# Loading x alone first, ten sigmoid tiles, weight means moved into the layer norm, one set of banks, and VectorE in the first two Sobel pairs

## The chip, the core and the metric

The kernel runs on one core of one Trainium2 chip. A core has a matrix engine (TensorE, called PE in the profile), a vector engine (VectorE, DVE), a scalar engine (ScalarE, ACT) and a general engine (GpSimd, POOL). SyncE (SP) only issues DMA transfers here. Every engine works off its own queue of instructions in order, and waits on semaphores for the others. TensorE writes its products to PSUM, which holds eight banks of 128 partitions by 512 float32. The metric is the device time of one execution in microseconds (us). All data is float32.

## The reference

Four layers on one image x of 256 x 256 pixels with 32 channels, each with its residual:

```python
x = x + attention(_gn(x))   # layer 0
x = x + sobel(_gn(x))       # layer 1
x = x + sobel(_gn(x))       # layer 2
x = x + recurrent(_gn(x))   # layer 3
```

`_gn` normalizes 16 groups of two channels over the whole image. `attention` normalizes each pixel over its 32 channels (mean, variance, `ln_gamma`, `ln_beta`), and then makes `q`, `k`, `v` and `g = sigmoid(mn @ Wg)` with 256 columns each. The softmax runs over an axis of length 1, so its weights are 1, and what is left is

```python
o = g * (mn @ Wv)
return o @ Wo + bo
```

`sobel` takes a 3 x 3 average (edges divided by the number of pixels that count), the two 3 x 3 Sobel gradients per channel, and `sqrt(gx*gx + gy*gy + 1e-6)`. `recurrent` takes the rows of the image as 256 sequences of 256 steps with 32 features, and runs two LSTM-like cells of 128 units with a group norm (four groups, `gn_gamma`, `gn_beta`) on the 512 gate inputs of each cell. For inputs whose `gn_gamma` is all ones and `gn_beta` all zeros the kernel takes a branch without these factors; a test of the two arrays sets `flag`, by which the branch is chosen.

## The kernel before

The image lies in SBUF as `xa`: 128 partitions are four neighbouring columns of the image (J = 4) times 32 channels, and the free side is 64 blocks (NB) of 256 rows. Work goes by *pairs* of blocks (128 x 512 elements), 32 of them (NST). From the load to the end of the Sobel layers the order of the instructions on each engine is the order in which the program writes them (`manual_schedule`); no scheduler moves them.

*Load.* SP loads x in natural layout into tiles `nat` and `half` (WIDTHS: two of 16 columns, then seven of 32; two DMAs each). TensorE transposes 128 x 128 pieces into PSUM (`pt`), ScalarE copies each pair into `xa` (L254), VectorE takes its statistics (`bn_stats`, L255). ScalarE's queue loads `kg` (two 128 x 128 matrices: group averaging and channel centring) and `mean_of`; GpSimd's queue loads the weights, `ln_gamma` and `ln_beta`, four times over. In the last third of the load `weights()` puts four narrow products and two of 128 x 256 on TensorE: the bias that `ln_beta` gives, and the centred weights `wv4` and `wg4`.

*Group norm and layer norm.* `bn_aggr`, two products with `kg` that average over a group (`pm`, `pv`), and from them `less` (minus the mean) and `scale`. `shifted(k)` subtracts the mean from a pair (mostly VectorE, L284). Eight groups of four pairs follow: TensorE centres each over channels (`pc`, L346), ScalarE squares (L369), TensorE sums the squares into `pvar` (L327). ScalarE's square root and VectorE's reciprocal (L360 for the first group of pairs, L376 for the others) make `rstd`. `rows_of(k)` has SP spread row `k` of `rstd` over 128 partitions, in four DMAs of 64 KB into one of three `rows` buffers (L305); `scaled(k)` multiplies a pair by it (pair 0 on VectorE, others on GpSimd, L315). `norm_test` (L744 to L747) compares `gn_gamma` and `gn_beta`, laid out on one partition, and writes `flag`. PSUM is split into a pool of seven banks for `pc` and one for `pvar`.

*Attention.* A list `plan` gives each step of a pair a planned time, with 5.9 between pairs; all pairs' entries, sorted by planned time, are the program. Per pair: eight products with `wv` (v) and eight with `wg` (g) on TensorE in 32-row slices (L441), eight sigmoids on ScalarE (`sg`, L450), eight times `o = (v + bias) * sg` on VectorE (L454), two groups of four products with `wo` (`pr`, `pb`, L467) into one bank, ScalarE's copy `r` with the bias `bo` (L482), GpSimd's addition into `xa` (L483), and `bn_stats` (L486). Banks are taken first in, first out from a list of eight; `sg` tiles from a list of eight and `o` tiles from a list of eleven. `spread_out` (the rows' DMAs) of pair k is planned five pairs ahead, `scaled` two pairs ahead.

`RecurrentWeights` is created where the attention starts: SP loads `wc` (2 x 512 KB, L758), GpSimd clears `bc` (L762), SP loads a row of it (L763). Its `centring()` gives a list of small instructions, one of which is put into each pair of the attention: reduces on VectorE (L809, L813: means of `bc` and `wc` by gate group) and subtractions on GpSimd (L816).

*Sobel layers.* A list `parts` with planned times 3.6 apart, sorted in the same way. Per pair: `convert` (ScalarE, into PSUM), `twos` and `threes` (VectorE, L586, L601), `ends` (ScalarE), then on GpSimd `fours` (L606), `difference` (L614) and `smooth` (L610), then two groups of products on TensorE (`mixed`, L648), squares, sum, root, residual and statistics. At the head of a layer `shift()` makes the group mean and then has TensorE multiply 16 idle products (L561); `deviation()` makes the scale.

*Recurrence.* 256 steps over two cells, with the weights that `rw.finish` makes ready. The change leaves it as it is.

Of the kernel before, what the change touches and what calls it, by code (L numbers as in the profile page):

```python
# [18 lines left out]
S = 256  # L19
T = 256  # L20
C = 32
# [40 lines left out]
def net_kernel(  # L62
# [35 lines left out]
    nc.scalar.dma_start(out=kg, in_=consts[:, 0:2, :])  # L98
# [18 lines left out]
    gamma4 = cp.tile([P, 1], F32, name="gamma4")  # L117
    beta4 = cp.tile([P, 1], F32, name="beta4")
    wv4 = big2.tile([P, D], F32, name="wv4")
    wg4 = big2.tile([P, D], F32, name="wg4")  # L120
    for t, v in (
        (wv4, w_v),
        (wg4, w_g),
        (gamma4, ln_gamma.rearrange("(c o) -> c o", o=1)),
        (beta4, ln_beta.rearrange("(c o) -> c o", o=1)),
    ):
        for j in range(J):
            nc.gpsimd.dma_start(out=t[j * C : (j + 1) * C, :], in_=v)
# [8 lines left out]
    one = eps_tile(1.0, "one")  # L137
# [52 lines left out]
    mean_of = mp.tile([P, P], F32, name="mean_of")  # L190
    nc.scalar.dma_start(out=mean_of, in_=consts[:, K_AVG, :])
    flag = cp.tile([1, 1], mybir.dt.int32, name="flag")
    stats = new_stats()
    def pair(t, k):
        return t[:, 2 * k : 2 * k + 2, :].rearrange("p b s -> p (b s)")
# [3 lines left out]
    WIDTHS = [16, 16] + 7 * [32]  # L199
    w0 = 0  # L200
    with tc.tile_pool(name="nat", bufs=7, side="right") as natp, tc.tile_pool(
        name="ps_in", bufs=5, space=PSUM
    ) as ps_in:
        nats = []
        for i, wl in enumerate(WIDTHS):
            name, bufs = ("nat", 7) if wl == 32 else ("half", 2)
            nat = natp.tile([P, 2, wl, C], F32, name=name, bufs=bufs)
            nats.append((nat, w0, wl))
            for h in range(2):
                nc.sync.dma_start(out=nat[:, h], in_=x_nat[:, h, w0 : w0 + wl, :])  # L210
            w0 += wl
        nc.sync.dma_start(out=kt, in_=consts[:, 3:NK, :])
        gb = norm_weights(tc, mp, gn_gamma, gn_beta)
        nc.gpsimd.memset(avg, 0.0)
        for g in range(GROUPS):
            nc.gpsimd.tensor_copy(avg[:, g, g, :], mean_of[:, 0:P:C])
        scaled_w = []
        for w in (wv4, wg4):
            scaled_w.append(mp.tile([P, D], F32, name="wgam", bufs=2))
            nc.gpsimd.tensor_scalar(scaled_w[-1], w, gamma4, None, ALU.mult)  # L220

        def weights():

            pbias = ps_in.tile([P, 2, 2, P], F32, name="pt")
            for i, w in enumerate((wv4, wg4)):
                for half in range(2):
                    nc.tensor.matmul(
                        pbias[:, i, half, 0:1],
                        lhsT=w[0:C, half * P : (half + 1) * P],
                        rhs=beta4[0:C, :],  # L230
                        start=True,
                        stop=True,
                    )
            nc.scalar.copy(wbias, pbias[:, :, :, 0:1].rearrange("p i h o -> p i (h o)"))
            for w, wg in zip((wv4, wg4), scaled_w):
                pw = ps_in.tile([P, 2, 2, P], F32, name="pt")
                pw = pw[:, 0].rearrange("p h s -> p (h s)")
                nc.tensor.matmul(pw, lhsT=kg[:, K_CEN, :], rhs=wg, start=True, stop=True)
                nc.scalar.copy(w, pw)

        for i, (nat, w0, wl) in enumerate(nats):
# [14 lines left out]
            if i == len(nats) - 3:  # L256
                weights()
# [6 lines left out]
    with tc.tile_pool(name="ps_gn", bufs=1, space=PSUM) as ps_gn:  # L264
        mv = small.tile([P, nc.vector.BN_AGGR_DIM], F32, name="mv")
        nc.vector.bn_aggr(mv, stats)
        busy(ps_gn, 5)
        pm = ps_gn.tile([P, 1], F32, name="pm")
        nc.tensor.matmul(pm, lhsT=kg[:, K_GN, :], rhs=mv[:, 0:1], start=True, stop=True)
        less = small.tile([P, 1], F32, name="less")  # L270
        nc.vector.tensor_scalar_mul(less, pm, -1.0)
        d = small.tile([P, 1], F32, name="d")
        nc.vector.tensor_add(d, mv[:, 0:1], less)
        q = small.tile([P, 1], F32, name="q")
        nc.vector.scalar_tensor_tensor(q, d, d, mv[:, 1:2], ALU.mult, ALU.add)
        pv = ps_gn.tile([P, 1], F32, name="pv")
        nc.tensor.matmul(pv, lhsT=kg[:, K_GN, :], rhs=q, start=True, stop=True)
        busy(ps_gn, 3)
        nc.scalar.activation(pair(xb, 2), pair(xa, 2), AF.Identity, bias=less)
        gstd = small.tile([P, 1], F32, name="gstd")  # L280
        nc.scalar.activation(gstd, pv, AF.Sqrt, bias=gn_eps)

        def shifted(k):
            nc.vector.tensor_scalar(pair(xb, k), pair(xa, k), one, less, ALU.mult, ALU.add)  # L284

        shifted(0)
        shifted(1)
        scale = small.tile([P, 1], F32, name="scale")
        nc.vector.reciprocal(scale, gstd)
        nc.vector.tensor_scalar(cen, kg[:, K_CEN, :], scale, None, ALU.mult)  # L290
        shifted(3)
        for w in (wv4, wg4):
            nc.scalar.activation(w, w, AF.Copy, scale=scale)

    def pair(t, k):
        return t[:, 2 * k : 2 * k + 2, :].rearrange("p b s -> p (b s)")
# [20 lines left out]
    with tc.tile_pool(name="lnq", bufs=9) as lnq:  # L317
        with tc.tile_pool(name="ps_ln", bufs=7, space=PSUM) as ps_ln, tc.tile_pool(
            name="ps_var", bufs=1, space=PSUM
        ) as ps_var:  # L320
            pvars = []

            def variance(g, sqs):
                if g in (0, EARLY):
                    pvars.append(ps_var.tile([P, 2 * S], F32, name="pvar"))
                for j in range(J):
                    nc.tensor.matmul(  # L327
                        pvars[-1][j * C : (j + 1) * C, :],
                        lhsT=avg[:, g].rearrange("p k j -> p (k j)"),
                        rhs=sqs[j],  # L330
                        start=g in (0, EARLY),
                        stop=g in (EARLY - 1, GROUPS - 1),
                    )

            def deviations():
                std = lnq.tile([P, 2 * S], F32, name="std", bufs=1)
                nc.scalar.activation(std, pvars[-1], AF.Sqrt, bias=ln_eps)
                return std

            last = std = None  # L340
            for g in range(GROUPS):
                pcs = [ps_ln.tile([P, 2 * S], F32, name="pc") for _ in range(J)]
                for j in range(J):
                    rows = slice(j * C, (j + 1) * C)
                    for r in range(J):
                        nc.tensor.matmul(  # L346
                            pcs[j][r * C : (r + 1) * C, :],
                            lhsT=cen[rows, rows],
                            rhs=pair(xb, J * g + r)[rows],
                            start=True,  # L350
                            stop=True,
                        )
                if g == 0:
                    for k in range(J, 5 * J):
                        shifted(k)
                sqs = []
                for j, pc in enumerate(pcs):
                    if g == EARLY + 1 and j == 1:
                        std = deviations()
                        nc.vector.reciprocal(rstds[0], std)  # L360
                        for k in range(3):
                            rowsets[k] = rows_of(k)
                        for k in range(5 * J, NST):
                            shifted(k)
                        norm_test(tc, mp, flag, gb)
                        for k in range(3):
                            scaled(k)
                    sqs.append(lnq.tile([P, 2 * S], F32, name="sq"))
                    nc.scalar.activation(sqs[-1], pc, AF.Square)  # L369
                if g:  # L370
                    variance(g - 1, last)
                last = sqs
            variance(GROUPS - 1, last)
            std = deviations()
            table(AF.Sigmoid, std[:, 0:1])
            nc.vector.reciprocal(rstds[1], std)  # L376

    means.close()
    rw = RecurrentWeights(tc, cells, one, w_cell, b_cell)
# [38 lines left out]
        (22.5883, "bn", 0, 0),  # L418
    ]
    with tc.tile_pool(name="at", bufs=3) as atp, tc.tile_pool(  # L420
        name="ps_at", bufs=1, space=PSUM
    ) as ps_at:
        free = list(range(8))
        held, sbuf = {}, {}
# [85 lines left out]
        for _, f, args in todo:  # L510
            f(*args)
# [756 lines left out]
```

## Time and profile before

| | us |
|---|---|
| median of 3 runs | 2520.72 (2519.58 to 2522.09) |
| the profiled execution's own time | 2522.59 |
| its span in the profile | 2520.8 |
| PE busy in the span | 2476.7 (98%) |
| DVE busy | 2273.3 (90%) |
| ACT busy | 2256.1 (89%) |
| POOL busy | 1332.8 (53%) |

By stages, in us from the start of the span (busy time of each engine in the stage; the clock is the mean TensorE clock that was granted, 1 being full speed):

| stage | from, to | PE | DVE | ACT | POOL | clock |
|---|---|---|---|---|---|---|
| load | 0, 33 | 23.75 | 20.40 | 20.68 | 16.78 | 1.00 |
| group and layer norm | 33, 59 | 23.04 | 23.71 | 19.97 | 0.00 | 1.00 |
| attention | 59, 303 | 237.03 | 200.69 | 188.21 | 89.60 | 0.96 |
| Sobel, first | 303, 425 | 121.84 | 106.97 | 87.72 | 97.27 | 1.00 |
| Sobel, second | 425, 549 | 123.94 | 107.91 | 87.38 | 97.92 | 1.00 |
| group norm, weights | 549, 560 | 9.43 | 7.35 | 3.80 | 0.36 | 1.00 |
| recurrence | 560, 2520.8 | 1937.66 | 1806.30 | 1848.30 | 1030.88 | 0.99 |

In the lines of a timeline, the first number is the start of a run of like instructions on one engine, the second their busy time, then come the engine, the line of the program, the operation, output and inputs with their shapes, and how many there are. In square brackets stands how long the engine was idle before, and what ended the idle time: the engine, the tile and the line that it waited for. "SPq" is SP's queue, where DMAs are issued. A busy PE need not be PE at its peak: a matmul is shown from its start to its modelled end.

### The profile page before, as it was taken

Reading aid. Unit: us, or ns where it says so; the run is one execution under the profiler, and the core shown is the slowest. Engines: PE = TensorE matmul, PEld = TensorE weight load, DVE = VectorE, ACT = ScalarE, POOL = GpSimd, SP = SyncE. Lnnn points to the kernel's source line nnn. Section 1 sums busy time; section 2 is a strip of 40 time slices with the busy share of each in tenths; the row PEclk is TensorE's granted clock in tenths of the full one; section 3 lists DMA queues with packets and bytes.
Section 4 is the critical chain, followed back from the end, with each engine's and each line's share of the span. In section 5 each row is a group of like instructions: output and inputs, shape, how many; then the busy total and the mean of one; then the engine's idle time right before and its main releaser. Section 6 shows DMA issues by size and latency. Waiting matters only on the chain.

```text
span 2520.8 us, 41461 instructions
## 1 busy us (share of the span) xinstructions
PE 2476.7 (98%) x11593; PEld 1062.3 (42%) x11593; DVE 2273.3 (90%) x6635; ACT 2256.1 (89%) x6878; POOL 1332.8 (53%) x1368
## 2 busy tenths in 40 slices
PE   7999999999999999999999999999999999999997
PEld 4444445563444444444444444444444444444442
DVE  7688897977999999999999999999999999999996
ACT  6788676758999999999999999999999999999996
POOL 2334487854555555555555555555555555555553
PEclk9899999998999999999999999999999999999998
DMA  6777100010010101010100101010101010100000
GB/s 163 60 38 39 8 1 1 1 39 13 5 22 5 22 5 22 5 24 8 21 15 12 22 5 22 5 22 5 22 5 22 5 22 5 22 5 5 5 7 9
DMA packets 117449, 46.98 MB, mean 19 GB/s; under 512 B 76964, under 2 KB 110021, under 8 KB 117208
## 3 DMA queue, kind: packets, MB, share of 16 engines
q1 hardware_dynamic: 115032, 43.60, 13.0%
q8 instruction: 95, 1.56, 0.3%
q14 instruction: 146, 1.20, 0.2%
q10 hardware_dynamic: 1376, 0.33, 0.1%
q0 software_dynamic: 800, 0.30, 0.1%
HBM read 10.63 MB, written 8.39 MB: 8 GB/s over the span
## 4 chain that ended last, share of the span: by engine, by line
PE 76%; DVE 0%; ACT 0%; issue 0%; POOL 0%; POOLq 0%; ACTq 0%; DVEq 0%
PE zz L1086 37%; PE zz L1081 17%; PE zz L1054 9%; PE pt L1138 5%; PE zz L1051 3%; PE pt L1134 2%; PE px L1183 1%; PE px L1173 1%; POOL rs L1102 0%; DVE ve L1099 0%; ACT ga L1075 0%; ACT sq L1094 0%; PE px L1166 0%; DVE c L1122 0%; ACT go L1075 0%
## 5 line engine op out<-in xcount | busy, mean ns | idle before, releaser
L1102 POOL TENSOR_TENSOR rs<-ve,mhalf 128x4 f32<-128x4 f32 x1024 | 1030.9, 1007 | 924.7 <-DVE ve L1099 924.7
L1086 PE MATMUL zz<-wc,hT 128*128 128x512 f32 x2040 | 1060.4, 607 | 0.7 <-DVE hT L1144 0.7
L1075 ACT ACTIVATE ga<-zz,rs 128x128 f32<-128x128 f32 x3072 | 972.8, 377 | 39.8 <-POOL rs L1102 10.9
L1099 DVE TENSOR_REDUCE ve<-sq 128x4 f32<-128x516 f32 x1024 | 703.4, 687 | 33.1 <-ACT sq L1094 9.8
L1094 ACT ACTIVATE sq<-zz 128x512 f32<-128x512 f32 x1024 | 629.0, 614 | 41.8 <-PE zz L1086 18.2
L1081 PE MATMUL zz<-wc,hT 128*128 128x512 f32 x1024 | 525.9, 595 | 0.0
L1086 PEld LDWEIGHTS zz<-wc,hT 128*128 128x128 f32 x2040 | 328.9, 190 | 399.5 <-DVE c L1130 167.6
L1075 ACT ACTIVATE go<-zz,rs 128x128 f32<-128x128 f32 x1024 | 393.9, 385 | 0.0
L1122 DVE TENSOR_TENSOR c<-ga 128x128 f32<-128x128 f32 x1024 | 299.0, 292 | 61.9 <-ACT ga L1075 31.1
L1130 DVE TENSOR_TENSOR c<-c,fc 128x128 f32<-128x128 f32 x1020 | 287.8, 282 | 9.0
L1126 DVE TENSOR_TENSOR fc<-ga,c 128x128 f32<-128x128 f32 x1020 | 291.9, 286 | 2.7 <-ACT ga L1075 2.7
L1054 PE MATMUL zz<-fx,xt 32*128 32x512 f32 x2048 | 266.3, 590 | 0.0
L450 ACT ACTIVATE sg<-pa,wbias 128x512 f32<-128x512 f32 x256 | 167.6, 686 | 52.9 <-DVE o L454 30.5
L454 DVE SCALAR_TENSOR_TENSOR o<-pa,wbias,sg 128x512 f32<-128x512 f32 x256 | 177.6, 743 | 31.9 <-ACT sg L450 20.7
L1138 PEld LDWEIGHTS pt<-ident,c 128*128 128x128 f32 x512 | 71.2, 139 | 284.5 <-DVE c L1130 274.9
L441 PE MATMUL pa<-xb,wg 32*128 32x512 f32 x512 | 165.5, 662 | 6.1 <-POOL xb L315 3.7
L1141 ACT ACTIVATE th<-c 128x128 f32<-128x128 f32 x512 | 166.2, 325 | 0.4 <-DVE c L1130 0.4
L1141 ACT ACTIVATE th<-pt 128x128 f32<-128x128 f32 x512 | 145.9, 285 | 18.6 <-PE pt L1138 18.6
L1081 PEld LDWEIGHTS zz<-wc,hT 128*128 128x128 f32 x1024 | 161.2, 197 | 2.8 <-issue 0.5
L1144 DVE TENSOR_TENSOR hT<-pt,th 128x128 f32<-128x128 f32 x512 | 145.9, 285 | 15.9 <-ACT th L1141 15.8
L441 PE MATMUL pa<-xb,wv 32*128 32x512 f32 x512 | 157.3, 651 | 0.0
L1134 PEld LDWEIGHTS pt<-ident,go 128*128 128x128 f32 x512 | 71.7, 140 | 202.8 <-ACT go L1075 201.8
(190 smaller groups left out, 2894.8 us busy)
## 6 DMA issues: line engine op xcount, KB each, us to landing
xt<-xa SPq DMA_DIRECT2D x256, 64.0 KB, 2.0
rows<-rstd SPq DMA_DIRECT2D x128, 64.0 KB, 6.5
out_dram<-st SPq DMA_DIRECT2D x252, 32.0 KB, 1.7
nat<-in_x_dram SPq DMA_DIRECT2D x14, 512.0 KB, 10.5
half<-in_x_dram SPq DMA_DIRECT2D x4, 256.0 KB, 4.6
wc<-in_L_conv_W_cell_dram SPq DMA_DIRECT2D x2, 512.0 KB, 6.0
kt<-in_consts_dram SPq DMA_DIRECT2D x1, 640.0 KB, 11.5
kg<-in_consts_dram ACTq DMA_DIRECT2D x1, 128.0 KB, 3.6
```

The costliest lines, as they stand in the source:

```text
L441: nc.tensor.matmul(take((o, u, j, k)), lhsT=w[rows, u * P : (u + 1) * P], rhs=pair(xb, k)[rows], start=True, stop=True,)
L1054: nc.tensor.matmul(v["zz", l, h, t], lhsT=inputs.of(t, r), rhs=fx[r, :], start=False, stop=l == 0 and t == 0,)
L1075: nc.scalar.activation(dst, gates(x, g), func, scale=scale)
L1081: nc.tensor.matmul(get("zz"), lhsT=v["hT", 0, t][:, seqs], rhs=wc[:, l, 0, :], start=False, stop=t == 0)
L1086: nc.tensor.matmul(get("zz"), lhsT=v["hT", l, t - 1][:, seqs], rhs=wc[:, l, 1, :], start=False, stop=True,)
L1094: nc.scalar.activation(sqs[l, h, t % 2][:, :, 0:H], four(get("zz")), AF.Square, scale=float(H**-0.5))
L1099: nc.vector.tensor_reduce(ve, sqs[l, h, t % 2], AX.X, ALU.add)
L1102: nc.gpsimd.tensor_tensor(rs, get("ve"), inputs.mhalf, ALU.pow)
L1122: nc.vector.tensor_mul(c, gates(get("ga"), 0), gates(get("ga"), 2))
L1126: nc.vector.tensor_mul(fc, gates(get("ga"), 1), get("c"))
L1130: nc.vector.tensor_add(c, c, get("fc"))
L1141: nc.scalar.activation(th, get("pt")[:, 1, 0:P] if turned else get("c"), AF.Tanh)
```

## The change

It has five parts.

1. *Load.* All loads but x's leave the front: `kg`, the two weights (one copy of 32 rows each), `ln_gamma`, `ln_beta`, `gn_gamma`, `gn_beta` (now over 128 partitions), `kt`, `wc` and `bc` are issued on SP behind x. `mean_of` is worked out from `ident` and `kg` on GpSimd. The last tile of x is split into two halves. TensorE gets 7 + 3 + 3 idle products. The products of the weights move to the group norm, where they stand behind `pv` in place of three idle products.
2. *Norm test.* It is cut into a comparison, a total (a product over partitions) and a decision, all in the group norm.
3. *One set of banks.* Group norm, layer norm and attention use one pool of eight tagged banks; the attention's list starts in the order 4, 5, 6, 0, 1, 2, 3, 7.
4. *Weight means.* `RecurrentWeights` is created in the load. The reduces stand in the layer norm, where `norm_test` stood; one subtraction goes into each pair of the attention. The list of `sg` tiles has ten entries.
5. *Sobel.* `fours` and `smooth` of the first two pairs run on VectorE. `twos`, `threes`, `ends`, `difference`, `fours` and `smooth` of these pairs come first in the program; `convert(1)` goes ahead of them, `deviation()` behind the second `twos`, and `difference` of pairs 2 to 5 ahead of their `fours`.

```diff
-    nc.scalar.dma_start(out=kg, in_=consts[:, 0:2, :])
...
-    for t, v in (
-        (wv4, w_v),
-        (wg4, w_g),
-        (gamma4, ln_gamma.rearrange("(c o) -> c o", o=1)),
-        (beta4, ln_beta.rearrange("(c o) -> c o", o=1)),
-    ):
-        for j in range(J):
-            nc.gpsimd.dma_start(out=t[j * C : (j + 1) * C, :], in_=v)
...
-    nc.scalar.dma_start(out=mean_of, in_=consts[:, K_AVG, :])
...
-    WIDTHS = [16, 16] + 7 * [32]
+    WIDTHS = [16, 16] + 6 * [32] + [16, 16]
...
+        nc.sync.dma_start(out=kg, in_=consts[:, 0:2, :])
+        for t, v in (
+            (wone[0], w_v),
+            (wone[1], w_g),
+            (gamma, ln_gamma.rearrange("(c o) -> c o", o=1)),
+            (beta, ln_beta.rearrange("(c o) -> c o", o=1)),
+        ):
+            nc.sync.dma_start(out=t, in_=v)
+        count = mp.tile([1, 1], F32, name="count")
+        compare, total_same, decide = norm_test(tc, mp, count, gn_gamma, gn_beta)
         nc.sync.dma_start(out=kt, in_=consts[:, 3:NK, :])
-        gb = norm_weights(tc, mp, gn_gamma, gn_beta)
+        rw = RecurrentWeights(tc, cells, one, w_cell, b_cell)
+        reduces, subtractions = rw.centring()
+        wgam = []
+        for w in wone:
+            wgam.append(mp.tile([C, D], F32, name="wgam", bufs=2))
+            nc.gpsimd.tensor_scalar(wgam[-1], w, gamma, None, ALU.mult)
...
+        nc.gpsimd.tensor_sub(mean_of, ident[:, 0:P:C], kg[:, K_CEN, 0:P:C])
...
+        busy_here(7)
...
-            if i == len(nats) - 3:
-                weights()
+            if i < 2:
+                busy_here(3)
...
+    nc.tensor.matmul(pv, lhsT=kg[:, K_GN, :], rhs=q, start=True, stop=True)
+    pbias = bank(3)
+    for i, w in enumerate(wone):
+        for half in range(2):
+            nc.tensor.matmul(
+                pbias[:, 2 * i + half : 2 * i + half + 1],
+                lhsT=w[:, half * P : (half + 1) * P],
+                rhs=beta,
...
+    compare()
+    psame = bank(6)[0:1, 0:1]
+    total_same(psame)
+    pws = [bank(4 + i)[:, 0:D] for i in range(2)]
+    for pw, w in zip(pws, wgam):
+        nc.tensor.matmul(
+            pw, lhsT=cen4.rearrange("c j k -> c (j k)"), rhs=w, start=True, stop=True
+        )
...
+    decide(psame, flag)
+    nc.scalar.copy(wbias, pbias[:, 0:4].rearrange("p (i h) -> p i h", i=2))
+    for w, pw in zip((wv4, wg4), pws):
+        nc.scalar.activation(w, pw, AF.Copy, scale=scale)
...
-                        norm_test(tc, mp, flag, gb)
+                    for f in reduces:
+                        f()
...
-    rw = RecurrentWeights(tc, cells, one, w_cell, b_cell)
...
-        free = list(range(8))
+        free = [4, 5, 6, 0, 1, 2, 3, 7]
...
-        slots = {name: list(range(n)) for name, n in (("sg", 8), ("o", 11))}
+        slots = {name: list(range(n)) for name, n in (("sg", 10), ("o", 11))}
...
-            (k * step + 6.0, lambda f=f: f(), ()) for k, f in enumerate(rw.centring())
+            (k * step + 6.0, lambda f=f: f(), ()) for k, f in enumerate(subtractions)
...
+        def fill(k):
+            return nc.vector if k < 2 else nc.gpsimd
...
-            nc.gpsimd.tensor_add(w, pp[:, :, 0 : S + 1], pp[:, :, 1 : S + 2])
+            fill(k).tensor_add(w, pp[:, :, 0 : S + 1], pp[:, :, 1 : S + 2])
...
-            nc.gpsimd.tensor_add(along[0][:, ring(k), :], w[:, :, 0:S], w[:, :, 1 : S + 1])
+            fill(k).tensor_add(along[0][:, ring(k), :], w[:, :, 0:S], w[:, :, 1 : S + 1])
...
+        early = [twos, threes, ends, difference, fours, smooth]
+
+        def moved(when, k, part):
+            if k < 2 and part in early:
+                return 0.1 * early.index(part) + 0.25 * k
+            if k == 1 and part is convert:
+                return -0.5
+            if 2 <= k < 6 and part is difference:
+                return k * every + 4.39
+            return when
+
+        todo = [(moved(when, k, part), k, part, args) for when, k, part, args in todo]
...
-                if part is twos and k == 0:
+                if part is twos and k == 1:
                     deviation()
...
```

`norm_test` after the change; `RecurrentWeights.centring` is the same but returns the reduces and the subtractions as two lists:

```python
def norm_test(tc, pool, count, gn_gamma, gn_beta):
    ...
    def compare():
        for i, value in enumerate((1.0, 0.0)):
            nc.vector.tensor_scalar(gb[:, i, :], gb[:, i, :], value, None, ALU.is_equal)
        nc.vector.tensor_reduce(same, gb.rearrange("p k m -> p (k m)"), AX.X, ALU.add)

    def total(ps):
        nc.tensor.matmul(ps, lhsT=same, rhs=ones, start=True, stop=True)

    def decide(ps, flag):
        nc.vector.tensor_scalar(count, ps, float(2 * L * G), None, ALU.is_equal)
        nc.vector.tensor_copy(flag, count)
```

## The prediction

> **What bounds the kernel now.** I began with the busy time by stages. From 560 us on the recurrence runs, which no edit touches; its 1961 us are left out below. What can move is the 560 us ahead of it: load (0 to 33), group and layer norm (to 59), attention (to 303), two Sobel layers (to 549). Then the timeline of each.
>
> The attention's steady state, one pair of blocks per 6.95 us:
>
> ```profile
> 269.88 4.23 DVE L454 SCALAR_TENSOR_TENSOR o<-pa,wbias,sg 128x512 f32<-128x512 f32 x6 [0.81 <-ACT sg L450]
> 270.73 1.29 ACT L450 ACTIVATE sg<-pa,wbias 128x512 f32<-128x512 f32 x2 [0.88 <-DVE o L454]
> 272.63 4.17 ACT L450 ACTIVATE sg<-pa,wbias 128x512 f32<-128x512 f32 x6
> 275.22 1.07 PE L467 MATMUL pa<-o,wo 128*32 128x512 f32 x8
> 276.22 0.69 PE L441 MATMUL pa<-xb,wg 32*128 32x512 f32 x1
> 276.83 4.23 DVE L454 SCALAR_TENSOR_TENSOR o<-pa,wbias,sg 128x512 f32<-128x512 f32 x6 [0.81 <-ACT sg L450]
> 277.68 1.29 ACT L450 ACTIVATE sg<-pa,wbias 128x512 f32<-128x512 f32 x2 [0.88 <-DVE o L454]
> ```
>
> ScalarE and VectorE wait for each other once a pair: the last sigmoid of six (ends 276.80) lets VectorE begin `o`; that first `o` (0.74) frees the sigmoid tile that ScalarE waits for (277.68). 6.07 of ScalarE's own work + 0.88 = 6.95.
>
> The attention's start:
>
> ```profile
> 68.25 1.26 POOL L315 TENSOR_TENSOR xb<-xb,rows 128x512 f32<-128x512 f32 x1 [4.50 <-DMA rows<-rstd]
> 69.46 0.94 POOL L762 MEMSET bc<- 33x1024 f32 x1
> 70.42 0.25 SPq L763 DMA_DIRECT2D bc<-in_L_conv_b_cell_dram  x1
> 71.86 0.68 DVE L809 TENSOR_REDUCE bm<-bc 33x4 f32<-33x512 f32 x1 [9.89 <-DMA bc<-in_L_conv_b_cell_dram]
> 72.46 1.39 DVE L454 SCALAR_TENSOR_TENSOR o<-pa,wbias,sg 128x512 f32<-128x512 f32 x2
> 80.87 1.27 POOL L315 TENSOR_TENSOR xb<-xb,rows 128x512 f32<-128x512 f32 x1 [10.47 <-PE pa L441]
> ```
>
> SP's load of `bc` waits for GpSimd's memset, which stands behind the scaling of pair 2. VectorE's first reduce waits for that load, all `o` queue behind the reduce, and the rows of pair 3 are issued after it on SP (70.72), so pair 3 is scaled at 80.87. (The wait put down to PE there I read as the rows' landing: PE had read that pair long before.) TensorE runs at half clock meanwhile:
>
> ```profile
> 74.00:78.00 4.00, 4.00 (x17) 2.92 (x14) 2.79 (x5) 2.16 (x4) 0.00 (x0) 0.50 0.74 37
> 86.00:90.00 4.00, 4.00 (x35) 1.65 (x32) 3.37 (x5) 2.70 (x6) 1.81 (x2) 1.00 0.83 43
> ```
>
> (after the stretch: its length, busy us of PE, PEld, DVE, ACT, POOL; the third number from the end is the clock). Four later pairs carry a reduce of `wc`; GpSimd's addition shows their spacing, 7.54 us instead of 6.95:
>
> ```profile
> 145.06 1.27 POOL L483 TENSOR_TENSOR xa<-xa,r 128x512 f32<-128x512 f32 x1 [4.03 <-ACT r L482]
> 152.60 1.27 POOL L483 TENSOR_TENSOR xa<-xa,r 128x512 f32<-128x512 f32 x1 [5.04 <-ACT r L482]
> ```
>
> Load: VectorE's statistics run back to back, stop for 0.65 us, and end the stage at 32.65. Sobel: TensorE's 16 idle products end at 313.30, and the first real ones follow at once, though their input (312.78) was ready:
>
> ```profile
> 18.16 9.00 DVE L255 BATCH_NORM_STATS2 stats<-xa 128x6 f32<-128x512 f32 x15 [0.16 <-ACT xa L254]
> 27.81 4.84 DVE L255 BATCH_NORM_STATS2 stats<-xa 128x6 f32<-128x512 f32 x8 [0.65 <-ACT xa L254]
> 306.15 7.15 PE L561 MATMUL pg<-kg,ident 128*128 128x256 f32 x32
> 311.74 1.04 POOL L614 TENSOR_TENSOR dh<-pp 128x512 f32<-128x512 f32 x1
> 313.23 1.51 PE L648 MATMUL pg<-dh,kt 128*64 128x256 f32 x11
> ```
>
> **The change, part by part** (times on the old timeline).
>
> *Load.* 0.45 MB of `kg`, `mean_of`, `wv` and `wg` leave x's path (1.1 us at the 404 GB/s of 18 to 20 us), and the weight products (24.61 to 26.7 on PE) leave the queue ahead of the last transposes. The last two tiles are halves: two copies, not four, follow the last landing. Statistics bound it: 28 of 0.605 us behind the third tile. Before, they began at 13.89 and the first five came 0.85 apart. If that tile lands 1.5 earlier and the pace holds, the stage ends 1.6 earlier; with no slow start (the warming products), 3.4. I take 2.7, between, nearer to the second since the 0.65 stop goes too. On SP, x is followed by `kg`, the small weights, `gb`, `kt`, `wc`, `bc`: 1.9 MB, some 5 us, landed before 35; `kg` is needed at 31, GpSimd's three products of it at 36. That is covered by the statistics.
>
> *Group and layer norm.* The two norm comparisons and a sum (three small VectorE operations at 0.16 to 0.19: 0.5 us) stand ahead of the first shifts, so the scale and `cen` (36.38) come 0.5 later. On PE, `pbias` (1.05 for eight passes in the load), the total and the two weight products (1.13) replace 1.54 of idle products: `pc` starts at about 37.5, not 36.71. ScalarE is the bound after that (32 squares of 0.50 from 38.03 to 56.75), so 0.8 stays; two more small VectorE operations (`decide`) push the first reciprocal 0.1 more. +0.9; bounds 0.2 (products hidden) and 1.6 (both delays added). The moved reductions cost VectorE 6 x 0.675 + 0.32 = 4.37 where the old test took 3.69 and was followed by 0.75 of waiting for rows: covered. One set of banks: the second group's products wait for ScalarE's read of the weights, done before its squares; nothing.
>
> *Attention's start.* Without the reduce, VectorE's first `o` can begin when the pair's third sigmoid ends and its v is there, 68.4 instead of 72.46. Rows of pair 3 now wait for pair 1's scaling (63.75) and not for `bc`. Rows come 5.5 us apart when nothing holds them (57.2, 62.4, 68.2), so pair 3 is scaled by 74.8, 7.3 earlier. At full clock: pair 2's first product at 69.57, unchanged, plus one period (6.83) plus 5.5 from a pair's first g to the r three pairs before (273.39 to 278.86) gives the first r at 81.9 instead of 88.66: -6.8. At half clock throughout, five groups of four products, `pr` and `pb` take 2.13 each from 71.2: 86.6, -2.1. I take -4.5, the middle: neither row is nearer.
>
> TensorE was busy for all of 74 to 78 and kept 0.50. [...]
>
> *Reductions gone from steady state.* Four pairs at 7.55 and one at 7.03 return to 6.95: -2.4.
>
> *Ten sigmoid tiles.* Each sigmoid waits two `o` further back, so 0.88 goes from that place. What is late next: the sigmoid's own product. It follows, in PE's order, the group that waits for the sixth `o` (274.11), then `pr` (275.22 to 276.28), then its own group (276.22, ends 277.35): ScalarE can start at 277.40, not 277.68. The ring is now: sixth `o` end, 3.29 to the sigmoid, 6.10 to the last sigmoid of six, 0.03, then 4.23 for six `o`: 13.65 over two pairs, 6.83 each. Below lies VectorE alone (4.23 + 0.68 + 1.39 = 6.30), above 6.954. 30 spacings x 0.12 = -3.6; ends 0 and -19.6; the value next to the PE rows is taken.
>
> *Sobel.* VectorE takes four additions, but the 16 idle products still end at 313.30. Only PE's 0.2 us gap ahead of the second pair (315.66 to 315.87) can go: -0.2 per layer, -0.4; ends 0 and -1. VectorE's four extra (0.69 each) lie in its idle 4.15 us ahead of 317.65.
>
> Sum: -2.7 + 0.9 - 4.5 - 2.4 - 3.6 - 0.4 = -12.7. The profiled execution took 2522.59 (span 2520.8), 1.87 over the median 2520.72, so 2509.9 for it and 2508.0 for the median.
>
> **Rivals.**
> 1. *The sigmoid wait turns into an equal wait for PE.* For: PE's records fill the period, and its start at 277.40 is only 0.28 under the old one. Against: two-pair ring above. Then 6.954 stays: 2508.0 + 3.6 = 2511.6.
> 2. *VectorE becomes the bound.* If the PE chain shifts forward with the rest, 6.30 per pair: -19.6 instead of -3.6, 2492. Against: `pr` and the group before it hold their place in the order.
> 3. *Slower: TensorE stays at half clock into the steady state.* At half clock six groups of 2.13 make 12.8 us a pair, 5.9 more than now. For: the clock did not return in 74 to 78. It decides from 12.7 / 5.9 = 2.2 further pairs; three give 2508.0 + 17.7 = 2525.7. Against: it returned at 86 with the first `pr`, and that comes earlier now.
> 4. *The start gains nothing* (half clock and rows no sooner) and the load only 1.6, with rival 1: 0.9 - 1.6 - 2.4 = -3.1, 2517.6: no change that counts.
>
> **How the numbers follow.** Forecast 0.60 (2503 to 2511), rival 1 0.17, rival 2 0.08, rival 4 0.08, rival 3 0.05, the rest 0.02 slower still. A measurement tells 0.2%, 5 us. Faster: 0.60 + 0.17 + 0.08 and a quarter of rival 4 = 0.87; same 0.07; slower 0.06. The range leaves out rival 2, rival 3 and the far part of 4: 2499 to 2516.
>
> **What would show it.** Right: ScalarE's idle per pair goes from 0.88 to some 0.6 and now names PE, spacing near 6.83 and alternating; no 7.54; no wait for `bc` in VectorE; first r near 82.4 (88.66 less 4.5 and less the 1.8 of the stages before); statistics end near 30; first Sobel products right behind the 16 idle ones. Wrong: a stretch of clock 0.50 after the first r; spacing of 6.95 or 6.3; `pc` starting over 2 us later after the group mean; or the recurrence's span off by more than 2 us.

## The result and the profile after

The changed kernel takes 2505.63 us, median of 5 runs (2501.73 to 2508.56), against 2520.72 (2519.58 to 2522.09, also 5 runs): a ratio of 0.994, 95% interval 0.9926 to 0.9955, 15.1 us less. Forecast were 2508.0, in a range of 2499 to 2516. The profiled execution of the changed kernel took 2504.49, its span is 2502.6.

By stages, in the two profiled executions (us; the aggregate is `bn_aggr` of a stage's statistics, the reciprocals are those of `rstd`):

| from, to | before | after | difference | forecast |
|---|---|---|---|---|
| start, first aggregate | 32.69 | 30.60 | -2.09 | -2.7 |
| first aggregate, second reciprocal | 25.93 | 30.22 | +4.30 | +0.9 |
| second reciprocal, first r | 30.04 | 22.57 | -7.47 | -4.5 |
| first r, last r | 210.81 | 202.87 | -7.94 | -6.0 |
| last r, first Sobel aggregate | 4.16 | 4.16 | 0 | 0 |
| first Sobel aggregate, second | 123.04 | 122.83 | -0.21 | -0.2 |
| second Sobel aggregate, first rs of the recurrence | 139.69 | 139.41 | -0.28 | -0.2 |
| from there to the end | 1954.46 | 1949.96 | -4.50 | 0 |
| sum | 2520.8 | 2502.6 | -18.2 | -12.7 |

In the last row the code is the same, and TensorE's granted clock differs: at the head of the recurrence it was 0.50 for 13.65 us before (from 567.22) and for 6.83 after (from 553.05), at the end for 3.41 and 14.8 us before (from 2499.17 and 2506.00) and for 14.2 after (from 2488.40). The -0.28 in the row above it is no gain of the second Sobel layer: that layer took 126.02 us from its aggregate to the next one both before and after, and the whole row was anything from 138.05 to 140.49 in the profiles below that keep the 16 idle products. Of the ten profiles of the experiments below, seven took 194.1 to 194.9 us from the first `rs` there to the 101st, like before (194.94), and three 192.8 to 193.0, like after (192.74), with the same code.

The steady state, in the timeline of the changed kernel:

```profile
256.98 4.21 DVE L472 SCALAR_TENSOR_TENSOR o<-pa,wbias,sg 128x512 f32<-128x512 f32 x6 [0.63 <-ACT sg L468]
261.21 0.69 PE L459 MATMUL pa<-xb,wv 32*128 32x512 f32 x1
262.30 1.06 PE L485 MATMUL pa<-o,wo 128*32 128x512 f32 x8
263.30 0.69 PE L459 MATMUL pa<-xb,wg 32*128 32x512 f32 x1
264.58 1.26 ACT L468 ACTIVATE sg<-pa,wbias 128x512 f32<-128x512 f32 x2 [0.88 <-PE pa L459]
266.64 3.80 ACT L468 ACTIVATE sg<-pa,wbias 128x512 f32<-128x512 f32 x6 [0.22 <-PE pa L459]
270.48 4.21 DVE L472 SCALAR_TENSOR_TENSOR o<-pa,wbias,sg 128x512 f32<-128x512 f32 x6 [0.63 <-ACT sg L468]
```

ScalarE's wait now names PE. The ring of the prediction is there: the sixth `o` ends at 261.19, its group of products starts at 261.21, then `pr` (262.30), the next group (263.30), the sigmoid (264.58), the last of six sigmoids (ends 270.44), `o` (270.48). That is twice 6.755 us, and all spacings but the last two have it. The pairs that carried a reduction before now show it too, at GpSimd's addition:

```profile
144.94 1.28 POOL L501 TENSOR_TENSOR xa<-xa,r 128x512 f32<-128x512 f32 x1 [3.81 <-ACT r L500]
151.69 1.27 POOL L501 TENSOR_TENSOR xa<-xa,r 128x512 f32<-128x512 f32 x1 [3.81 <-ACT r L500]
```

The start of the attention:

```profile
64.15 1.26 POOL L338 TENSOR_TENSOR xb<-xb,rows 128x512 f32<-128x512 f32 x1 [32.26 <-DMA rows<-rstd]
69.44 1.26 POOL L338 TENSOR_TENSOR xb<-xb,rows 128x512 f32<-128x512 f32 x1 [4.03 <-PE pa L459]
71.16 0.75 DVE L472 SCALAR_TENSOR_TENSOR o<-pa,wbias,sg 128x512 f32<-128x512 f32 x1 [6.99 <-PE pa L459]
74.67 1.27 POOL L338 TENSOR_TENSOR xb<-xb,rows 128x512 f32<-128x512 f32 x1 [3.54 <-DMA rows<-rstd]
```

No wait for `bc` is left. Pairs 1, 2 and 3 are scaled 5.2 to 5.3 us apart, and the first `r` is at 83.39. The granted clock, by stretches (the columns as before, the clock is the third number from the end; the five busy times are those of PE, PEld, which is TensorE's loading of weights, DVE, ACT and POOL):

```profile
30.80:34.20 3.40, 2.62 (x19) 2.04 (x17) 2.67 (x10) 1.03 (x3) 1.03 (x8) 1.00 0.75 280
34.20:37.60 3.40, 3.40 (x38) 1.55 (x37) 3.33 (x12) 1.06 (x3) 0.00 (x0) 0.50 0.01 2
37.60:41.00 3.40, 3.40 (x52) 1.01 (x39) 3.40 (x8) 2.81 (x6) 0.00 (x0) 0.50 0.02 5
41.00:44.40 3.40, 3.40 (x40) 0.37 (x32) 1.59 (x4) 1.22 (x3) 0.00 (x0) 0.50 0.00 0
44.40:47.80 3.40, 2.11 (x56) 0.43 (x40) 1.95 (x1) 2.64 (x5) 0.00 (x0) 0.99 0.01 2
```

Here lies the loss: the kernel before had 1.00 from 17.7 to 62; the changed one runs the head of its layer norm at half clock (0.50 from 34.22 to 44.46), and the first reciprocal starts 15.26 us after the aggregate instead of 11.37.

The end of the load, before, and then load and Sobel after:

```profile
22.82 1.86 PE L247 MATMUL pt<-ident,nat 128*128 128x128 f32 x15 [0.67 <-DMA nat<-in_x_dram]
24.61 0.60 PE L227 MATMUL pt<-beta,wv 32*128 32x1 f32 x4
25.08 0.58 PE L227 MATMUL pt<-beta,wg 32*128 32x1 f32 x4
25.59 1.13 PE L238 MATMUL pt<-wgam,kg 128*128 128x256 f32 x4
26.55 3.66 PE L247 MATMUL pt<-ident,nat 128*128 128x128 f32 x32
```

```profile
24.51 1.86 PE L243 MATMUL pt<-ident,nat 128*128 128x128 f32 x15 [0.92 <-DMA nat<-in_x_dram]
25.71 4.85 DVE L251 BATCH_NORM_STATS2 stats<-xa 128x6 f32<-128x512 f32 x8 [0.93 <-ACT xa L250]
...
292.96 7.15 PE L580 MATMUL pg<-kg,ident 128*128 128x256 f32 x32
295.92 1.35 POOL L636 TENSOR_TENSOR dh<-pp 128x512 f32<-128x512 f32 x1 [0.31 <-ACT xp L601]
300.05 1.51 PE L670 MATMUL pg<-dh,kt 128*64 128x256 f32 x11
```

VectorE's last eight statistics wait 0.93 us, at the end for x itself. The part of x that they begin with (columns 192 to 223) landed at 24.47, and they start 1.24 us later; in the kernel before it landed at 25.47, and they started at 27.81, 2.34 later, since the weight products stood ahead of its transposes on TensorE. In the Sobel layer the second difference is there at 297.27, but the 16 idle products hold TensorE until 300.05.

### The profile page after: what moved, and what is told of

Its sections match the earlier page's. It is cut to its first block, busy times and chain, and to the rows that moved or that the text cites. A ratio compares the mean times of both kernels' runs of the same rounds, so it can differ in the third digit from the quotient of the medians.

```text
span 2502.6 us, 41399 instructions
## 1 busy us (share of the span) xinstructions
PE 2462.8 (98%) x11615; PEld 1057.6 (42%) x11615; DVE 2276.8 (91%) x6644; ACT 2247.5 (90%) x6876; POOL 1318.6 (53%) x1347
## 4 chain that ended last, share of the span: by engine, by line
PE 77%; DVE 0%; ACT 0%; POOL 0%; issue 0%; DVEq 0%; POOLq 0%; ACTq 0%
PE zz L1135 37%; PE zz L1130 17%; PE zz L1103 9%; PE pt L1187 5%; PE zz L1100 3%; PE pt L1183 2%; PE px L1232 1%; PE px L1222 1%; POOL rs L1151 0%; DVE ve L1148 0%; ACT ga L1124 0%; ACT sq L1143 0%; PE px L1215 0%; DVE c L1171 0%; DVE fc L1175 0%
## 5 line engine op out<-in xcount | busy, mean ns | idle before, releaser
L468 ACT ACTIVATE sg<-pa,wbias 128x512 f32<-128x512 f32 x256 | 160.1, 685 | 44.9 <-PE pa L459 40.2
L459 PE MATMUL pa<-xb,wg 32*128 32x512 f32 x512 | 157.7, 649 | 3.5 <-POOL xb L338 3.5
L1199 DVE COPY hT<-pt 128x128 f32<-128x128 f32 x512 | 145.1, 283 | 8.9 <-PE pt L1187 8.9
```

## The experiments

Medians and ratios are of the timed runs, against 2520.9 to 2521.8 us of the kernel before, measured beside each; ways and spacings are from one profiled execution of each kernel.

### Ten tiles, undone and alone

```diff
-        slots = {name: list(range(n)) for name, n in (("sg", 10), ("o", 11))}
+        slots = {name: list(range(n)) for name, n in (("sg", 8), ("o", 11))}
```

> The changed kernel with eight sigmoid tiles again and nothing else. My theory: the eight tiles alone set the spacing of 6.954 us before, so it returns: r to r 6.95 instead of 6.755, ScalarE's idle time of some 0.9 us a pair names o again and not PE, first to last r grows by 30 x 0.2 = 6.0 us, about 2511.6 us in all. Rival, the new order of the banks or the reductions moved out of the attention made the spacing: it stays within 0.03 of 6.755, and the time within 2 us of 2505.6.

> The kernel before with ten sigmoid tiles and nothing else. My theory: the spacing of pairs that carry no reduction of wc goes from 6.954 to 6.755 us (what the changed kernel shows), with the old order of banks too; the four pairs with a reduction stay 0.4 to 0.6 longer; first to last r shrinks by 5 to 6 us, about 2515 us. By the sum in the prediction it would be 6.83 and -3.6. Rival, the tiles matter only together with the new bank order: 6.95 stays and the time within 1 us of before.

The changed kernel with eight tiles: 2511.99 us (ratio 0.9964, 0.9951 to 0.9977), spacing 6.96, first to last r 208.51 (+5.64). The kernel before with ten: 2513.22 (0.9966, 0.9954 to 0.9978), spacing 6.755, first to last r 204.54 (-6.27). ScalarE with eight tiles, then VectorE and ScalarE with ten in the kernel before:

```profile
268.53 1.29 ACT L468 ACTIVATE sg<-pa,wbias 128x512 f32<-128x512 f32 x2 [0.88 <-DVE o L472]
270.43 4.18 ACT L468 ACTIVATE sg<-pa,wbias 128x512 f32<-128x512 f32 x6
```

```profile
264.78 1.26 ACT L450 ACTIVATE sg<-pa,wbias 128x512 f32<-128x512 f32 x2 [0.88 <-PE pa L441]
266.85 3.80 ACT L450 ACTIVATE sg<-pa,wbias 128x512 f32<-128x512 f32 x6 [0.23 <-PE pa L441]
```

The tiles alone carry the spacing, with either order of banks. Six sigmoids in a row took 4.18 us with eight tiles and 3.80 with ten: part of what I read as ScalarE's own work was waiting. Inside the line of 4.17 us of the kernel before lie two pauses of 0.11 to 0.12 us (ahead of 274.01 and 275.46), and the sigmoids behind a wait for VectorE start 0.65 to 0.80 us after the one before them, where it takes 0.58 without such a wait. With ten tiles the four pairs with a reduction of `wc` are 0.33 to 0.43 us longer, not 0.60.

### The half clock in the layer norm

```diff
     nc.tensor.matmul(pm, lhsT=kg[:, K_GN, :], rhs=mv[:, 0:1], start=True, stop=True)
+    busy_ln(2)
...
+    busy_ln(3)
     pbias = bank(3)
```

> The changed kernel with five idle products put back in the group norm: two behind pm, three behind pv. The changed kernel ran at half clock from 34.2 to 44.5 us, and its way from the aggregate to the second reciprocal was 30.2 us instead of 25.9. My theory: too few full products in the 3.4 us before 34.2, since narrow ones took the place of idle ones. Then the clock stays 1.00 through the layer norm, that way is 26.5 to 27.3 us, and the time 2.5 to 4 us under 2505.6. Rival, the weight products that stand ahead of pc on TensorE cost the time, whatever the clock: the way grows by the five products' 1.3 us to some 31.5, and the time by as much. Third: the half clock stays for another reason, and nothing or up to +2 us.

2505.31 us (0.9941, 0.9927 to 0.9954). The clock stayed full (1.00 from 31.0 to 48.0), and the way from aggregate to second reciprocal was 27.68 us:

```profile
31.00:34.40 3.40, 3.31 (x18) 2.49 (x16) 2.68 (x10) 0.98 (x2) 1.00 (x8) 1.00 0.74 275
34.40:37.80 3.40, 3.40 (x49) 2.15 (x48) 2.71 (x9) 1.07 (x3) 0.00 (x0) 1.00 0.01 2
37.80:41.20 3.40, 3.40 (x72) 0.99 (x70) 3.40 (x9) 3.25 (x7) 0.00 (x0) 1.00 0.02 5
```

The first two theories were half right each. The clock went with what TensorE was given there (0.50 without the five products, 1.00 with them), but they (0.447 us each, by 7.15 for 16 in the Sobel layer, not the 0.26 that I had taken) cost about as much as they save: the total is that of the changed kernel. What the half clock costs can be read from the other runs, which have the same code in this stage. It lasted 3.41 us in five runs (eight tiles, no idle products in the load, both with 10 idle products in Sobel, `bc` late) with ways of 27.00 to 27.29; 6.83 in one run (28.63); 10.24 in the profiled run of the changed kernel (30.22). That is 1.6 us for each 3.41, and leads to an estimate of 25.4 without any (27.0 - 1.6), which no run of this order showed; the 27.68 above less five products of 0.447 is 25.4 too.

### What held the attention's start

```diff
-        rw = RecurrentWeights(tc, cells, one, w_cell, b_cell)
-        reduces, subtractions = rw.centring()
...
+    rw = RecurrentWeights(tc, cells, one, w_cell, b_cell)
     stats = new_stats()
```

(and the reduces back into the attention's list); in the second kernel only the clearing, load and reduces of `bc`.

> The changed kernel with the recurrent weights created at the attention's start and their reduces spread over the attention again, as before; load, norms, banks and ten sigmoid tiles stay. My theory: VectorE's first o waits for the load of bc again and pair 3's rows behind it, so the way from the second reciprocal to the first r goes from 22.6 to 26 to 30 us, and the pairs with a reduction of wc are 0.4 to 0.6 us longer (1.6 to 2.4 in all); layer norm within 0.5 us; 2511 to 2515 us. Rival, the gain at the start was the clock's (two windows of half clock fewer) and not the wait for bc: the first r stays within 1 us, and the time grows by 2 us at most.

> The changed kernel with only bc late: its clearing, its load and its two reduces stand at the attention's start as before, while wc's loads and reduces stay in the load and the layer norm. With all of it late the first r came 44.4 us after the first reciprocal, as before, against 37.5 to 39.2 in the runs of the changed order. My theory: the wait for bc is the cause, so 43.5 to 45.5 us here, and 2510 to 2512 us in all, since the pairs of the steady state stay at 6.755. Rival, the 1 MB of wc that was loaded there held up the rows: then the first r stays at 37.5 to 39.5 us after the first reciprocal, and the time within 1.5 us of 2505.6.

All late: 2511.47 us (0.996, 0.9944 to 0.9975); first r 44.4 us after the first reciprocal, as before (44.6), against 37.5 to 39.2 in the runs of the changed order; first to last r 204.56 (+1.69). Only `bc` late: 2508.17 (0.9956, 0.9941 to 0.9971), less than I had expected, but 43.5 us to the first r, and spacing 6.755 throughout. The wait for `bc`, with only `bc` late:

```profile
68.94 0.31 SPq L818 DMA_DIRECT2D bc<-in_L_conv_b_cell_dram  x1
69.35 25.74 SPq L328 DMA_DIRECT2D rows<-rstd  x20
70.47 0.68 DVE L865 TENSOR_REDUCE bm<-bc 33x4 f32<-33x512 f32 x1 [9.45 <-DMA bc<-in_L_conv_b_cell_dram]
78.82 1.26 POOL L338 TENSOR_TENSOR xb<-xb,rows 128x512 f32<-128x512 f32 x1 [9.91 <-DMA rows<-rstd]
```

So the 4 KB of `bc` (two rows of 512), by their place in three queues, put off the first r by 4.3 to 6.0 us in these profiles; with the 1 MB of `wc` on the same queue it was 0.9 more. The medians are only 2.5 us apart, and the intervals of their ratios overlap. The clock went with the late `bc` as well: between the first reciprocal and the first r TensorE had half clock for 20.5 to 23.9 us in the four profiles with a late `bc` (43.5 to 45.5 us to the first r), for 6.8 in three of the changed order (37.5 to 37.7) and for 13.7 in three others (39.1 to 39.2). How much of the delay is the wait alone, these runs do not tell.

### Idle products of the load

```diff
-        busy_here(7)
...
-            if i < 2:
-                busy_here(3)
```

> The changed kernel without the 7 + 3 + 3 idle products of the load. The prediction made the slow early copies (0.85 us apart instead of 0.62) worth 1.8 us of the load. My theory now: in the changed kernel x's arrival bounds the load (VectorE waits 0.33 and 0.93 us for it), so slow early copies catch up: the aggregate starts within 0.9 us of 30.60, and the time within 1.5 us of 2505.6. Rival, the prediction's: the aggregate starts 1.5 to 2 us later, at 32.1 to 32.6.

2504.55 us (0.9932, 0.9917 to 0.9948), and the aggregate at 30.59, where the changed kernel has 30.60. The early copies were slow again (0.85 us apart), and from 15.46 on VectorE ran without a pause (25 statistics in 15.10 us) and caught up just as the last parts of x came; in the changed kernel it waited 0.93 us for them instead.

### Idle products of the Sobel layers

```diff
-    stats = sobel_layer(xa, xb, stats, 3, 16, [rw.selectors])
+    stats = sobel_layer(xa, xb, stats, 3, 10, [rw.selectors])
```

(the same in the second layer); in the second kernel also with the old order of the first two pairs.

> The changed kernel with 10 idle products instead of 16 at the head of each Sobel layer. In the changed kernel the first two differences are there 6.8 us after the aggregate begins, and the idle products end 9.6 us after it. My theory: the early parts were hidden by the idle products; 6 of them fewer (0.447 us each, 2.68) let the first real products start 6.9 to 7.3 us after the aggregate, and each layer takes 2.0 to 2.7 us less (120.1 to 120.8 from aggregate to aggregate instead of 122.83): 2500 to 2502 us in all. Rival, GpSimd's supply of the next pairs is late then and TensorE waits for it: under 1 us a layer.

> The changed kernel with the Sobel part undone, and with 10 idle products instead of 16. My theory: with the old order GpSimd has the second pair's difference only some 9.2 us after the aggregate begins, so the shorter idle stretch gives little: first real products 9 to 9.6 us after the aggregate or, if they start earlier, a wait behind them; aggregate to aggregate 122.3 to 123.2 us, and the time 3 to 5 us above the run with the new order and 10 products. Rival, the idle products alone were too many, whatever the order: 120 to 121 us here too, and the two runs agree within 1 us.

New order: 2501.32 us (0.9922, 0.9906 to 0.9937); first products 7.03 us after the aggregate, from aggregate to aggregate 120.80. Old order: 2502.1 (0.9932, 0.9916 to 0.9948), 7.02 and 121.87. The old order pays a wait behind its first products, which the new one hasn't:

```profile
294.95 1.51 PE L670 MATMUL pg<-dh,kt 128*64 128x256 f32 x10
296.06 1.04 POOL L636 TENSOR_TENSOR dh<-pp 128x512 f32<-128x512 f32 x1
297.15 0.64 PE L670 MATMUL pg<-dh,kt 128*64 128x512 f32 x1 [0.69 <-POOL dh L636]
```

The first expectation held, the second did not: 6 idle products fewer bring 2.03 us in the first layer in the new order (122.83 to 120.80), but 1.17 in the old one too (123.04 in the kernel before, to 121.87). With 10 of them the early parts are worth 1.07 us in the first layer and 0.87 in the second (123.94 to the next aggregate against 124.81), with 16 it was 0.21 and nothing. The two medians, 0.8 us apart with runs that spread over 7 us, are too coarse to show it.

### A version with the weight products behind the layer norm

Weight products and bias behind the layer norm, one idle product behind `pm` and three behind `pv`, three behind the weights, 10 in the Sobel layers, and another starting order of the banks; the second version has besides, ahead of the third pair's first product:

```diff
+        def idle(n):
+            junk = take("idle")
+            for _ in range(n):
+                nc.tensor.matmul(junk[:, 0:S], lhsT=ident, rhs=kg, start=True, stop=True)
+            release("idle")
+
+        todo.append((2 * step - 0.005, idle, (4,)))
```

> The changed kernel with the products of the weights and their bias moved from the group norm to behind the layer norm (TensorE and ScalarE wait there for rows), one idle product behind pm and three behind pv, three behind the weights, and 10 idle products instead of 16 in the Sobel layers. My theory: the clock stays full in the layer norm and no idle product there is in anybody's way: aggregate to second reciprocal 25 to 26 us (27.0 to 30.2 in the runs of the changed order, with one to three windows of half clock, 27.7 with five idle products). The first r follows the first reciprocal by about 37.5 us, since the rows' transfers set the pace from there: at 78.5 to 80 instead of 83.4. With 4 to 5 us from the Sobel layers: 2495 to 2499 us. Rival: the weight products delay the first g products and with them the first r, so that only the Sobel gain is left, about 2501 us; or half clock in the layer norm all the same.

> The version with the weight products behind the layer norm and 10 idle products in the Sobel layers, and besides with four idle products ahead of the third pair's first product, where TensorE waited 2.08 us for the rows and then ran at half clock for 10.2 us. My theory: the clock returns sooner or stays, and the first r, 39.6 us after the first reciprocal there, comes 1.5 to 3 us earlier, at 36.5 to 38 us after it; 2497.5 to 2500 us in all. Rival, the rows set the pace whatever the clock (they land 5.2 to 5.8 us apart): 39 to 40 us again and the same time within 1 us.

The first: 2500.85 us (0.9926, 0.9912 to 0.9939); full clock in the layer norm, 26.45 us to the second reciprocal, but the first r only at 82.79, since TensorE waited 2.08 us for the third pair's rows and then had half clock from 69.13 to 79.37. The second: 2499.6 us (0.9922, 0.9909 to 0.9936), first r at 79.44, 36.7 us after the first reciprocal instead of 39.6. The stretch in question, first without and then with the four products:

```profile
65.00:69.00 4.00, 1.92 (x15) 0.84 (x13) 2.07 (x3) 2.49 (x5) 1.69 (x2) 1.00 0.80 58
69.00:73.00 4.00, 4.00 (x19) 2.29 (x13) 0.95 (x2) 1.84 (x3) 1.00 (x1) 0.52 0.90 45
73.00:77.00 4.00, 4.00 (x16) 2.71 (x13) 3.27 (x5) 2.53 (x4) 0.69 (x2) 0.50 0.75 54
```

```profile
65.00:69.00 4.00, 4.00 (x25) 2.28 (x22) 2.07 (x3) 2.09 (x5) 1.70 (x2) 1.00 0.80 52
69.00:73.00 4.00, 4.00 (x18) 1.87 (x16) 2.14 (x4) 3.09 (x5) 0.90 (x1) 1.00 0.77 51
73.00:77.00 4.00, 4.00 (x26) 1.65 (x23) 3.22 (x5) 3.47 (x6) 0.79 (x2) 1.00 0.85 45
```

Here idle products paid, in a gap in which TensorE had waited 2.08 us: this is the only profile with no half clock between the first reciprocal and the first r, and 36.7 is the shortest way. It is one profile for each version, and the two medians, 1.25 us apart, don't tell them apart. The second version's median is 6.0 us under the changed kernel's; the intervals of the two ratios still touch (0.9909 to 0.9936 and 0.9926 to 0.9955).

## Why the prediction was right, and where not

The total was right: 2.4 us over the measured median, in the likeliest case's own range. Part of that is luck: in the sum, the layer norm was priced too low for the profiled execution, and the attention's start and the ten tiles too low as gains. One sign that was to show it wrong came, the recurrence's span off by more than 2 us (-4.50); by the profiles it goes with the clock there. Point by point:

- *Ten sigmoid tiles (-3.6).* Right in mechanism, shown by doing it alone and undoing it; the size was off. Of the ring's terms, 3.29 + 6.10 + 0.03 + 4.23, the second is 5.86 in the profile after (264.58 to 270.44), because the six sigmoids' 4.17 held hidden waiting; 3.39 + 5.86 + 0.04 + 4.21 = 13.50, so 6.755 and not 6.83. Measured: -5.64. (30 times 6.954 - 6.825 would have been -3.9.) I also expected an alternating spacing, and there is none; and ScalarE's idle time did not shrink to 0.6, it is 0.88 and 0.22 a pair, both now put down to PE. Rivals 1 (6.954 stays) and 2 (6.30) fall.
- *Reductions out of the steady state (-2.4).* Right: from before to the changed kernel with eight tiles, first to last r shrinks by 2.30.
- *Attention's start (-4.5) and layer norm (+0.9).* Their sum, -3.6, came out at -3.2, but as two errors that cancel in this execution; in the five other profiles with this start it was -4.7 to -5.9, so that the start was priced too low (-5.8 to -7.5 there). What was mis-sized is the middle between full clock (-6.8) and half clock throughout (-2.1; as written, seven steps of 2.13 from 71.2 end at 86.1 and not at 86.6): from the first reciprocal to the first r, half clock fell from 20.5 us to 6.8, and the way from 44.60 to 37.54, 7.05 less. The start is also better counted from the first reciprocal, since by the program the rows of the first four pairs hang on it and not on the second; here the two moved almost alike (+3.88 and +4.30), which leaves 0.4 for that. The cause that I gave, `bc` ahead of VectorE's first `o` and of pair 3's rows, is shown, and the clock went with it.
- *The layer norm's step that failed* is "pbias, the total and the two weight products replace 1.54 of idle products", priced at full clock. With the idle products in those gaps the clock had been 1.00 (before, 31.4 to 48.4). In seven of seven profiles with that replacement there was half clock between 34 and 45 us, in neither of the two with the old order, and in none of the three with idle products in those gaps. With 3.41 us of half clock the term is +1.1, near the forecast; the profiled execution had 10.24, and +4.30. The bound of 1.6 was too low because no bound for the clock was in it, though I had written rival 3 about the clock one stage later.
- *Load (-2.7).* -2.09, in its bounds, but the reason given for going beyond 1.6 falls: the idle products bring nothing (30.59 without them). What is shown is the weight products' leaving TensorE's queue: from the landing of columns 192 to 223 to VectorE's last eight statistics it took 2.34 and 2.32 us in the two profiles with the old load, and 1.24 to 1.33 in the ten with the new, so 1.0 to 1.1 us. That x lands sooner is not shown: those columns landed at 25.47 and 24.60 with the old load and at 24.38 to 25.49 with the new. The kernel before with ten tiles had its aggregate at 31.80, not 32.69, with the same load, so some 0.9 of the -2.09 lies within what one execution differs from another.
- *Sobel (-0.4).* -0.21 in the first layer, as forecast, and nothing in the second (126.02 both times), where -0.2 was forecast. The reason given holds: the 16 idle products hid the rest, as cutting them shows.
- *Rival 3 (half clock into the steady state)* did not come: the clock was back at 71.8 in the profile after, and at 73.9 at the latest in the experiments that left the start as the change has it. Rival 4 falls with the start's gain.

## What to carry to other kernels

Where an idle or useful product is taken out of a gap, ask what the clock will do in the next few microseconds, and price it: here 1.6 us for each 3.41 us of half clock in the layer norm. With products of one column or of 32 rows in its place the clock fell to 0.50 here (after, from 34.22). Idle products were worth their place here where TensorE would have waited anyway (36.7 us to the first r instead of 39.6), and they have to be counted again when the work that they bridge moves: the Sobel part of this change gained 0.2 us in all until six of them were taken out of each layer. And count a start from the event that its first transfers wait for, not from the last event of the stage before.

## What was not expected

*How long the half clock lasted.* Apart from the end of the recurrence, the granted clock was 0.50 in the profile before for 6.83 us from 62.05, 13.65 from 72.29, 3.41 from 560.40 and 13.65 from 567.22; in the profile after, for 10.24 from 34.22, 6.83 from 64.94, 3.41 from 546.22 and 6.83 from 553.05. In the layer norm it lasted 3.41, 6.83 or 10.24 us in seven profiles with the same code there; what decided between them these runs do not show. The changed kernel's runs spread from 2501.73 to 2508.56 while the same program ran, and their mean granted clocks lie in the same order: 0.993 (2501.73), 0.992 (2504.49), 0.990 (2505.63), 0.989 (2508.20) and 0.988 (2508.56). Where in the program these runs differ is not shown, since only the one of 2504.49 was profiled.

*Busy and yet at half clock.* TensorE was busy throughout by the record in the three rows from 34.20 to 44.40 above and was granted 0.50. Nor did the busy share ahead of them tell what came here: the stretch from 30.80 to 34.20 was 2.62 of 3.40 us busy and 0.50 followed; that of the kernel before, from 31.40 to 34.80, was 2.66 busy and 1.00 followed. The two differ in the width of the products: full-width ones filled 0.8 us of the first (to 31.58; what follows is one column wide: `pm`, `pv`, the bias, the total) and 2.3 us of the second (to 33.69). With full-width products put back, 1.00 followed (five of them, from 34.40 to 48.00; one and three, in the second version above, from 31 to 57). No run tells whether the width alone decides it.
